# A decoder layer on one core: row maxima of a unit turned by a DMA, and other banks and another order for the background work

## The chip, the cores and the metric

The kernel runs on one core of a Trainium2 chip. The metric is the device time of one execution in microseconds (us), as the median of several executions. Beside it stands one profiled execution, whose trace shows every instruction of the five engines and every DMA. The engines are TensorE (PE in the profile, with its weight loads as PEld), VectorE (DVE), ScalarE (ACT), GpSimd (POOL) and SyncE (SP, which issues the DMAs).

## The reference

One decoder layer in float32 on x of 2 batches x 2048 rows x 512 columns, with 16 heads of width 32. Three sublayers follow each other, each adding to x:

```python
x = x + attn(layernorm(x)) @ W_o.T       # q, k, v by W_q, W_k, W_v; rotary positions on q and k
x = x + gelu(layernorm(x) @ ctx.T) @ ctx # ctx: 77 x 512 for each batch, gelu by tanh
x = x + clip((layernorm(x) @ sign(W).T) * scale + bias, -100, 100)
```

attn is softmax(q k^T / sqrt(32)) v for each head, without a mask, so that every query row meets all 2048 keys of its batch.

## The kernel before, in words

The batches are done one after the other. In each, `project_batch` goes over 16 chunks of 128 rows: layernorm, transpose, the products pk, pq and pv with the three weights (`times`, L179), the rotation (`rotate`), and the transposes of q and k (`transpose_qk`), so that q and k lie with a head's 32 columns on partitions. Then `Attention.run` goes over 32 units. A unit is 256 query rows of four heads, and has 8 steps; a step t takes two chunks of keys, and has two halves, one for heads 0 and 1, one for heads 2 and 3.

The softmax subtracts a row's maximum. These maxima are found ahead, by other matmuls than the ones that are weighed. In each half-step `maxima` (L400) computes two tiles ps of scores with queries on partitions (L412), ten steps ahead (AHEAD), and VectorE reduces them (L424). When a unit's 8 steps of maxima are there, `split_maxima` (L428) takes the negated maximum and splits it into three bf16 parts on GpSimd (casts L433, L435, L437), in a tile mt with queries on partitions. `turn_maxima` (L439) brings them into rows: two TensorE transposes ptm (L443) into a PSUM tile, and a VectorE copy to mrow (L445). The first matmul of a tile of scores, `lower` (L479), multiplies ones by mrow and so puts the negated maxima under the scores (L484; at steps 0 and 4 of each unit). Then come the scores with keys on partitions (L499), which add to what stands there, as the keys of a block are stored as differences to the block before. ScalarE takes the exponent (L625), GpSimd adds pairs for the sums (L627), and TensorE weighs the values (L517) and totals the sums (L531), one and two steps later. `divide` (L541) ends a unit at step 1 of the next: a ScalarE copy, then in each half a VectorE reciprocal (L551) and a GpSimd product.

What follows the attention, `after_attention` (L279), is a generator: output projection and sum with x (po, L293), statistics, the reciprocal root (`rstd_seed`, `rstd_step`), normalization and transpose (pt, L318), the context products (ph, L331; po, L350), the norm again, and the last projection (pf, L358) with scaling, clipping, sum and store. Each yield ends a piece. `background(n)` (L372) takes up to n pieces from the queue. In the attention it is called in the first half of every fourth step and in the second half of each (L635, L644), and in both halves of the last four units; in the projections of the second batch, three pieces at a time. What is left at the very end runs with all generators in turn, and then VectorE does what GpSimd did (`side`).

The order in the attention is the order in the code: a manual schedule covers TensorE, VectorE, ScalarE and GpSimd (L605). It doesn't cover SP, and it doesn't cover the projections and the end, where the planner orders the instructions. Each engine does its instructions in its own order, and so does SP, which holds loads of x, stores of the output and weights in one queue.

[...] ps_t (four, tag t) holds the tiles st of the scores and, in the projections, pt, pk and pq; ps_s (three, tag s) holds the maxima ps, the transposes of q and k, pv, ptm and all tiles of the background; ps_acc has one. A pool hands its banks out in turn, and a tile waits until the one that had its bank before is read.

In the last chunk of a batch (L250 to L270) the products are interleaved with the maxima that are still due (`lead`, L571).

Of the kernel before, what the change touches and what calls it, by code (L numbers as in the profile page):

```python
# [17 lines left out]
P = 128  # L18
B, S, D = 2, 2048, 512
H, DK = 16, 32  # L20
C = 77
# [16 lines left out]
def decoder_layer(  # L38
# [114 lines left out]
    def project_batch(b, ahead, att, wk, wq, wv):  # L153
# [25 lines left out]
        def times(dst, xnt, w, part=range(ND)):  # L179
            for i in part:  # L180
                nc.tensor.matmul(dst, xnt[:, i, :], w[:, i, :], start=(i == 0), stop=(i == ND - 1))  # L181
# [9 lines left out]
            if c == CPB - 1 and 1 in which:  # L191
                att.open_block(blk)

        def values(ch, xnt):
            pv = ps_s.tile([P, D], F32, tag="s", name="pv")
            times(pv, xnt, wv)
            v = kvq.tile([P, D], F32, tag=f"v{ch}", name=f"v_{b}_{ch}")
            nc.scalar.copy(v, pv)
            att.v.append(v)
# [50 lines left out]
        times(pk, xnt, wk)  # L250
        rotate(ch, 1, pk, r)
        transpose_qk(*held)
        values(ch - 1, left)
        transpose_qk(ch, r[:, 0], (1,))
        times(pq, xnt, wq, (0, 1))
        att.lead(1)
        times(pq, xnt, wq, (2, 3))
        rotate(ch, 0, pq, r)
        att.lead(1)
        pv = ps_s.tile([P, D], F32, tag="s", name="pv")  # L260
        times(pv, xnt, wv, (0, 1))
        att.lead(2 * AHEAD)
        times(pv, xnt, wv, (2, 3))
        v = kvq.tile([P, D], F32, tag=f"v{ch}", name=f"v_{b}_{ch}")
        nc.scalar.copy(v, pv)
        att.v.append(v)
        transpose_qk(ch, r[:, 0], (0,))
        att.split_maxima(0)
        att.turn_maxima(0)
# [6 lines left out]
    def side():  # L276
        return nc.vector if alone else nc.gpsimd

    def after_attention(b, blk, ot, first, end):  # L279
        wo, wf, fs, fb = late["wo"], late["wf"], late["fs"], late["fb"]  # L280
        ctxn, ctxt = late["ctx"]
        n = end - first
        chunks = [slice(c * P, (c + 1) * P) for c in range(first, end)]
        whole = slice(first * P, end * P)
        xs = [load_x(b, blk * CPB + c) for c in range(first, end)]
        yield


        def add_to_x(matmuls, mv):
            for c in range(n):  # L290
                ps = ps_s.tile([P, D], F32, tag="s", name="po")
                matmuls(ps, chunks[c])
                nc.vector.tensor_add(xs[c], ps, xs[c])  # L293
                yield
                chunk_stats(xs[c], mv[:, c, :])
                yield


        def norm(mv):
            v, y, t = rstd_seed(mv[:, :, 1], n)  # L300
            yield
            for _ in range(3):
                rstd_step(side(), v, y, t)
                yield
            off = small.tile([P, n], F32, tag=f"off{n}", name="off")
            side().tensor_mul(off, mv[:, :, 0], y)
            side().tensor_scalar(off, off, -1.0, None, ALU.mult)
            yield
            yield
            for c in range(n):  # L310
                xn = work.tile([P, D], F32, tag="w", name="xn2")
                nc.scalar.activation(
                    xn, xs[c], AF.Identity, bias=off[:, c : c + 1], scale=y[:, c : c + 1]
                )
                yield
                pt = ps_s.tile([P, ND, P], F32, tag="s", name="pt2")
                for i in range(ND):
                    nc.tensor.transpose(pt[:, i, :], xn[:, i * P : (i + 1) * P], ident)  # L318
                nc.scalar.copy(ot[:, :, chunks[c]], pt)
                yield  # L320

        def project_out(ps, cols):
            for i in range(ND):
                nc.tensor.matmul(ps, ot[:, i, cols], wo[:, i, :], start=(i == 0), stop=(i == ND - 1))  # L324

        mv = small.tile([P, n, 2], F32, tag=f"mv{n}", name="mv2")
        yield from add_to_x(project_out, mv)
        yield from norm(mv)
        ph = ps_s.tile([C, n * P], F32, tag="s", name="ph")
        for i in range(ND):  # L330
            nc.tensor.matmul(ph, ctxt[:, i, :], ot[:, i, whole], start=(i == 0), stop=(i == ND - 1))  # L331
        h = work.tile([C, n * P], F32, tag="w", name="h")
        nc.scalar.copy(h, ph)
        yield
        u = work.tile([C, n * P], F32, tag="w", name="u")
        side().tensor_mul(u, h, h)
        yield
        side().tensor_scalar(u, u, 0.044715, 1.0, ALU.mult, ALU.add)
        side().tensor_mul(u, u, h)
        yield  # L340
        yield
        nc.scalar.activation(u, u, AF.Tanh, scale=GELU_C)
        yield
        side().tensor_scalar(u, u, 1.0, 0.5, ALU.add, ALU.mult)
        side().tensor_mul(u, u, h)
        yield
        yield

        def attend_ctx(ps, cols):
            nc.tensor.matmul(ps, u[:, cols.start - whole.start : cols.stop - whole.start], ctxn, start=True, stop=True)  # L350

        mv = small.tile([P, n, 2], F32, tag=f"mv{n}", name="mv3")
        yield from add_to_x(attend_ctx, mv)
        yield from norm(mv)
        for c, cols in enumerate(chunks):
            pf = ps_s.tile([P, D], F32, tag="s", name="pf")
            for i in range(ND):
                nc.tensor.matmul(pf, ot[:, i, cols], wf[:, i, :], start=(i == 0), stop=(i == ND - 1))  # L358
            y = work.tile([P, D], F32, tag="w", name="y")
            nc.vector.tensor_mul(y, pf, fs)  # L360
            yield
            side().tensor_add(y, y, fb)
            yield
            side().tensor_scalar(y, y, -MAX_VAL, MAX_VAL, ALU.max, ALU.min)
            side().tensor_add(xs[c], xs[c], y)
            r0 = blk * BLK + (first + c) * P
            nc.sync.dma_start(out[b, r0 : r0 + P, :], xs[c])
            yield

    queue = []  # L370

    def background(n):  # L372
        while queue and n > 0:
            if next(queue[0], queue) is queue:
                queue.pop(0)
            else:
                n -= 1

    def drain():
# [6 lines left out]
    class Attention:  # L386
# [41 lines left out]
        def split_maxima(self, u):  # L428
# [7 lines left out]
            nc.gpsimd.tensor_tensor(neg, neg, mt[:, :, :, 1], ALU.subtract)  # L436
            nc.gpsimd.tensor_copy(mt[:, :, :, 2], neg)  # L437

        def turn_maxima(self, u):  # L439
            mt = mts[u % 2]  # L440
            pt = ps_s.tile([P, 2, P], BF16, tag="s", name="ptm")
            for c in range(2):
                nc.tensor.transpose(pt[:, c, :], mt[:, c].rearrange("p h d -> p (h d)"), ident_b)  # L443
            mrow = small.tile([P, HQ], BF16, tag="mrow", name="mrow")
            nc.vector.tensor_copy(mrow, pt.rearrange("p c q -> p (c q)"))  # L445
            self.mrow[u] = mrow

        def key_steps(self):  # L450
            self.dk = [None] + [
                const.tile([P, ND, BLK], F32, tag=f"w{n}", name=f"dk{n}") for n in "kqv"
            ]

            def differences(g):
                for kb in range(1, NB):
                    nc.gpsimd.tensor_sub(
                        self.dk[kb][:, g, :], self.k[kb][:, g, :], self.k[kb - 1][:, g, :]
                    )
                    yield  # L460

            def others():
                for g in range(1, ND):
                    for _ in differences(g):
                        for _ in range(4):
                            yield

            for _ in differences(0):
                pass
            queue.append(others())  # L470
# [107 lines left out]
        def run(self):  # L578
# [32 lines left out]
                }  # L611
            )
            ordered.__enter__()
            for t in range(NU * STEPS):
                u, i = divmod(t, STEPS)
                pw = big.tile([P, 4, 2, HQ], F32, tag="s", name="pw")
                sm = sums.tile([P, 4, HQ], F32, tag="sm", name="sm")
                for heads, others in (((0, 1), (2, 3)), ((2, 3), (0, 1))):
# [10 lines left out]
                        reduce()  # L629
                    if heads[0] == 0:  # L630
                        first_half()
                        if i == STEPS - 1 and u + 1 < NU:
                            self.turn_maxima(u + 1)
                        finish()
                        if t % 4 == 1 or u >= NU - ND:  # L635
                            background(1)
                    else:
                        finish()
                        second_half()
                        if prev is not None and prev[1] == STEPS - 1:  # L640
                            finish()
                        if (t + AHEAD) % STEPS == STEPS - 1 and u + 1 < NU:
                            self.split_maxima(u + 1)
                        background(1)  # L644
                prev = (u, i, pw, sm)
            first_half()
            second_half()
            while ends:
                finish()
            ordered.__exit__(None, None, None)  # L650

    for b in range(B):
# [60 lines left out]
```

## Time and profile before

| | us |
|---|---|
| median of 3 runs | 2842.28 (2841.74 to 2842.78) |
| profiled execution, its time | 2841.91 |
| profiled execution, its span | 2840.1 |
| TensorE busy in the span | 2800.2 |
| VectorE busy | 1722.5 |
| ScalarE busy | 1321.0 |
| GpSimd busy | 1805.7 |

The span runs from the first to the last instruction. A busy time is the union of an engine's instructions; a matmul's end is modelled, so a matmul that runs slowly and one that is held up can look alike. In the groups, a row names line, engine, operation and tiles, then the count, then busy us and mean ns of one, then the idle time of the engine ahead of it and what ended most of that. In the timeline, a row starts with its start and its duration in us; several like instructions that follow each other are merged, with their count. The granted clock of TensorE was 0.994 in the mean.

From the timeline: the projections of the first batch run to about 229 us, the attention of the first batch to about 1390, the projections of the second to about 1634, its attention to about 2793, and the rest to the end.

### The profile page before, as it was taken

To read this page: it belongs to the slowest core of one execution; us is meant where nothing else is said; L and a number is where in the kernel's file an instruction comes from. 1 tells how busy PE (TensorE), PEld (TensorE's weight loads), DVE (VectorE), ACT (ScalarE), POOL (GpSimd) and SP (SyncE) were. 2 spreads that over 40 slices of the span, in tenths; PEclk is the share of its full clock that TensorE was granted. 3 is DMA by queue.
4 is the path that set the end of the run, shared out by engine and by line. 5 is a ranking of instruction groups with operands and counts; after the bars stand their busy time and mean duration, and the time that the engine had idled before them with its cause. 6 is when DMAs were issued, how large, how long until landed. Compare 5 with 4: busy or idle time off the path is not lost.

```text
span 2840.1 us, 70979 instructions
## 1 busy us (share of the span) xinstructions
PE 2800.2 (99%) x30872; PEld 1494.3 (53%) x30872; DVE 1722.5 (61%) x3065; ACT 1321.0 (47%) x2391; POOL 1805.7 (64%) x2393
## 2 busy tenths in 40 slices
PE   8999999999999999999999999999999999999997
PEld 4445555555555555555444455555555555555554
DVE  4446767666666666665244467766766666666653
ACT  2114555455545544654321155555555455545552
POOL 4326767566856685767654277666677567756772
PEclk9999999999999999999999999999999999999998
DMA  4000000000000010000201000000000000000000
GB/s 135 22 15 1 2 2 2 2 2 9 24 2 2 2 32 1 2 5 28 71 23 34 12 2 2 2 2 2 2 17 17 1 2 9 24 2 2 16 9 15
DMA packets 24007, 39.50 MB, mean 14 GB/s; under 512 B 6902, under 2 KB 6902, under 8 KB 23696
## 3 DMA queue, kind: packets, MB, share of 16 engines
q1 hardware_dynamic: 23696, 34.98, 3.9%
q8 instruction: 241, 3.95, 0.6%
q14 instruction: 70, 0.57, 0.1%
HBM read 26.58 MB, written 8.39 MB: 12 GB/s over the span
## 4 chain that ended last, share of the span: by engine, by line
PE 94%; DVE 2%; POOL 2%; issue 1%; ACT 0%; DMA 0%; ACTq 0%; POOLq 0%; DVEq 0%
PE st L499 20%; PE acc L517 20%; PE ps L412 19%; PE acc L531 8%; PE pf L358 4%; PE po L324 4%; PE pv L181 4%; PE pq L181 4%; PE pk L181 4%; PE st L484 3%; PE pt L318 1%; PE po L350 1%; PE ph L331 1%; PE ptqk L189 1%; DVE mx L424 1%
## 5 line engine op out<-in xcount | busy, mean ns | idle before, releaser
L627 POOL TENSOR_TENSOR sm<-pw 128x512 f32<-128x512 f32 x1024 | 1299.0, 1272 | 665.7 <-ACT pw L625 663.6
L424 DVE TENSOR_REDUCE mx<-ps 128x1 f32<-128x512 f32 x2048 | 1311.6, 682 | 595.1 <-PE ps L412 569.2
L625 ACT ACTIVATE pw<-st 128x512 f32<-128x512 f32 x2048 | 1111.8, 595 | 1038.8 <-PE ps L412 702.5
L412 PE MATMUL ps<-k,q 32*128 32x512 f32 x4096 | 1244.4, 640 | 3.8 <-DVE mx L424 3.5
L517 PE MATMUL acc<-pw,v 128*32 128x256 f32 x8192 | 654.4, 391 | 0.0
L412 PEld LDWEIGHTS ps<-k,q 32*128 32x128 f32 x4096 | 371.7, 183 | 59.3 <-issue 25.8
L531 PE MATMUL acc<-sm,ones 128*32 128x128 f32 x7680 | 388.7, 280 | 1.3 <-POOL sm L627 1.3
L517 PEld LDWEIGHTS acc<-pw,v 128*32 128x32 f32 x8192 | 161.4, 108 | 420.6 <-issue 401.7
L531 PEld LDWEIGHTS acc<-sm,ones 128*32 128x32 f32 x7680 | 247.3, 110 | 156.0 <-POOL sm L627 2.0
L499 PE MATMUL st<-q,dkq 32*128 32x256 f32 x2048 | 294.0, 402 | 0.0
L499 PE MATMUL st<-q,dkk 32*128 32x256 f32 x2048 | 291.3, 400 | 0.0
L499 PE MATMUL st<-q,dkv 32*128 32x256 f32 x2048 | 291.0, 401 | 0.0
L499 PE MATMUL st<-q,k 32*128 32x256 f32 x2048 | 262.8, 374 | 0.0
L499 PEld LDWEIGHTS st<-q,dkk 32*128 32x128 f32 x2048 | 175.2, 184 | 99.5 <-issue 55.5
L499 PEld LDWEIGHTS st<-q,dkq 32*128 32x128 f32 x2048 | 171.3, 184 | 74.1 <-issue 50.9
L499 PEld LDWEIGHTS st<-q,dkv 32*128 32x128 f32 x2048 | 170.4, 184 | 62.6 <-ACT pw L625 26.1
L499 PEld LDWEIGHTS st<-q,k 32*128 32x128 f32 x2048 | 195.2, 187 | 14.2
L214 POOL TENSOR_TENSOR r<-r 128x512 f32<-128x512 f32 x64 | 81.1, 1270 | 184.0 <-DVE r L213 168.4
L293 DVE TENSOR_TENSOR x<-po,x 128x512 f32<-128x512 f32 x64 | 44.2, 691 | 132.4 <-PE po L324 97.7
L190 ACT COPY q<-ptqk 128x512 f32<-128x512 f32 x32 | 18.9, 591 | 221.6 <-PE ptqk L189 221.5
L551 DVE RECIPROCAL num<-num 128x128 f32<-128x128 f32 x128 | 120.5, 942 | 1.8 <-ACT num L545 1.8
L181 PE MATMUL pk<-wk,xnt 128*128 128x512 f32 x256 | 118.6, 606 | 2.0 <-ACT xnt L176 2.0
(100 smaller groups left out, 2085.6 us busy)
## 6 DMA issues: line engine op xcount, KB each, us to landing
x<-in_x_dram SPq DMA_DIRECT2D x64, 256.0 KB, 2.7
out_dram<-x SPq DMA_DIRECT2D x32, 256.0 KB, 2.0
wk<-in_wk_t_dram SPq DMA_DIRECT2D x2, 1024.0 KB, 5.2
wq<-in_wq_t_dram SPq DMA_DIRECT2D x2, 1024.0 KB, 10.1
wv<-in_wv_t_dram SPq DMA_DIRECT2D x2, 1024.0 KB, 9.5
wo<-in_wo_t_dram SPq DMA_DIRECT2D x1, 1024.0 KB, 7.0
wf<-in_wf_t_dram SPq DMA_DIRECT2D x1, 1024.0 KB, 9.0
ctx<-in_ctx_dram SPq DMA_DIRECT2D x2, 154.0 KB
```

The costliest lines, as they stand in the source:

```text
L181: nc.tensor.matmul(dst, xnt[:, i, :], w[:, i, :], start=(i == 0), stop=(i == ND - 1))
L324: nc.tensor.matmul(ps, ot[:, i, cols], wo[:, i, :], start=(i == 0), stop=(i == ND - 1))
L358: nc.tensor.matmul(pf, ot[:, i, cols], wf[:, i, :], start=(i == 0), stop=(i == ND - 1))
L412: nc.tensor.matmul(ps, self.q[qb][self.rows[h], g, q0 : q0 + P], self.k[kb][self.rows[h], g, :], start=True, stop=True,)
L424: nc.vector.tensor_reduce(mx[:, qc, h, kb : kb + 1], ps, AX.X, ALU.max)
L484: nc.tensor.matmul(self.st[h], ones_b[r, :], mrow[r, None, :].to_broadcast([DK, 2, HQ]), start=True, stop=False, skip_group_check=True,)
L499: nc.tensor.matmul(self.st[h][:, c, :], keys[r, g, kc * P : (kc + 1) * P], self.q[qb][r, g, hf * HQ : (hf + 1) * HQ], start=False, stop=Tr ...
L517: nc.tensor.matmul(acc[self.rows[h], 0, :], self.v[self.chunk(i, c)][:, d0 : d0 + DK], pw[:, h, c, :], start=(i == 0 and c == 0), stop=(i ...
L531: nc.tensor.matmul(acc[self.rows[h], 1, part], ones, sm[:, h, part], start=False, stop=(i == STEPS - 1), skip_group_check=True,)
L551: nc.vector.reciprocal(num[:, 1, part], num[:, 1, part])
L625: nc.scalar.activation(pw[:, h], self.st[h], AF.Exp, scale=SCALE)
L627: nc.gpsimd.tensor_add(sm[:, hs, :], pw[:, hs, 0, :], pw[:, hs, 1, :])
```

## The change

Four edits.

1. `turn_maxima` issues one DMA on SP's queue, which transposes both 128x128 bf16 blocks of mt straight to mrow. Only the first unit of each batch keeps the TensorE transposes and the VectorE copy. The call moves from the first half of step 7 to the second half of step 5, right behind `split_maxima`.
2. The tiles of the background come from `bank`: ps_s while the attention runs, ps_t otherwise, and at the very end the two in turn.
3. Each yield of the generator says whether the next piece begins with matmuls of the background. The first half of every odd step takes a piece only if it doesn't (`light`); the second halves and the last four units take any.
4. In the last chunk of a batch, one `lead` follows each of the four matmuls of pq; both pv tiles come from ps_t, and the last is computed in one go after all maxima.

```diff
-        def values(ch, xnt):
-            pv = ps_s.tile([P, D], F32, tag="s", name="pv")
+        def values(ch, xnt, pool=None):
+            pv = (pool or ps_s).tile([P, D], F32, tag="t" if pool else "s", name="pv")
...
-        values(ch - 1, left)
+        values(ch - 1, left, ps_t)
         transpose_qk(ch, r[:, 0], (1,))
-        times(pq, xnt, wq, (0, 1))
-        att.lead(1)
-        times(pq, xnt, wq, (2, 3))
+        for i in range(ND):
+            times(pq, xnt, wq, (i,))
+            att.lead(1)
         rotate(ch, 0, pq, r)
-        att.lead(1)
-        pv = ps_s.tile([P, D], F32, tag="s", name="pv")
-        times(pv, xnt, wv, (0, 1))
         att.lead(2 * AHEAD)
-        times(pv, xnt, wv, (2, 3))
-        v = kvq.tile([P, D], F32, tag=f"v{ch}", name=f"v_{b}_{ch}")
-        nc.scalar.copy(v, pv)
-        att.v.append(v)
+        values(ch, xnt, ps_t)
         transpose_qk(ch, r[:, 0], (0,))
...
+    attending = []
+    banks = [0]
+
+    def bank(shape, name):
+        banks[0] += 1
+        if attending or (alone and banks[0] % 2):
+            return ps_s.tile(shape, F32, tag="s", name=name)
+        return ps_t.tile(shape, F32, tag="t", name=name)
...
             for c in range(n):
-                ps = ps_s.tile([P, D], F32, tag="s", name="po")
+                ps = bank([P, D], "po")
                 matmuls(ps, chunks[c])
                 nc.vector.tensor_add(xs[c], ps, xs[c])
-                yield
+                yield False
                 chunk_stats(xs[c], mv[:, c, :])
-                yield
+                yield c + 1 < n
...
-                yield
-                pt = ps_s.tile([P, ND, P], F32, tag="s", name="pt2")
+                yield True
+                pt = bank([P, ND, P], "pt2")
...
-                yield
+                yield c + 1 == n
...
-    def background(n):
-        while queue and n > 0:
-            if next(queue[0], queue) is queue:
+    heavy = [False]
+
+    def background(n, light=False):
+        while queue and n > 0 and not (light and heavy[0]):
+            more = next(queue[0], queue)
+            if more is queue:
                 queue.pop(0)
+                heavy[0] = False
             else:
+                heavy[0] = more
                 n -= 1
...
         def turn_maxima(self, u):
             mt = mts[u % 2]
-            pt = ps_s.tile([P, 2, P], BF16, tag="s", name="ptm")
-            for c in range(2):
-                nc.tensor.transpose(pt[:, c, :], mt[:, c].rearrange("p h d -> p (h d)"), ident_b)
-            mrow = small.tile([P, HQ], BF16, tag="mrow", name="mrow")
-            nc.vector.tensor_copy(mrow, pt.rearrange("p c q -> p (c q)"))
-            self.mrow[u] = mrow
+            mrow = small.tile([P, 2, P], BF16, tag="mrow", name="mrow")
+            if u > 0:
+                nc.sync.dma_start_transpose(mrow, mt.rearrange("p c h d -> p (c h d)"))
+            else:
+                pt = ps_s.tile([P, 2, P], BF16, tag="s", name="ptm")
+                for c in range(2):
+                    nc.tensor.transpose(
+                        pt[:, c, :], mt[:, c].rearrange("p h d -> p (h d)"), ident_b
+                    )
+                nc.vector.tensor_copy(mrow, pt)
+            self.mrow[u] = mrow.rearrange("p c q -> p (c q)")
...
+            attending.append(True)
             for t in range(NU * STEPS):
...
                         first_half()
-                        if i == STEPS - 1 and u + 1 < NU:
-                            self.turn_maxima(u + 1)
                         finish()
-                        if t % 4 == 1 or u >= NU - ND:
+                        if u >= NU - ND:
                             background(1)
+                        elif t % 2 == 1:
+                            background(1, light=True)
...
                             self.split_maxima(u + 1)
+                            self.turn_maxima(u + 1)
                         background(1)
...
+            attending.clear()
```

More of the change, by code (lines that the diff above doesn't have):

```diff
@@ L285, in after_attention @@
         xs = [load_x(b, blk * CPB + c) for c in range(first, end)]
-        yield
+        yield True
         def add_to_x(matmuls, mv):
             for c in range(n):
-                ps = ps_s.tile([P, D], F32, tag="s", name="po")
+                ps = bank([P, D], "po")
                 matmuls(ps, chunks[c])
                 nc.vector.tensor_add(xs[c], ps, xs[c])
-                yield
+                yield False
                 chunk_stats(xs[c], mv[:, c, :])
-                yield
+                yield c + 1 < n
         def norm(mv):
             v, y, t = rstd_seed(mv[:, :, 1], n)
-            yield
+            yield False
             for _ in range(3):
                 rstd_step(side(), v, y, t)
-                yield
+                yield False
             off = small.tile([P, n], F32, tag=f"off{n}", name="off")
@@ L307, in norm @@
             side().tensor_scalar(off, off, -1.0, None, ALU.mult)
-            yield
-            yield
+            yield False
+            yield False
             for c in range(n):
@@ L314, in norm @@
                 )
-                yield
-                pt = ps_s.tile([P, ND, P], F32, tag="s", name="pt2")
+                yield True
+                pt = bank([P, ND, P], "pt2")
                 for i in range(ND):
@@ L319, in norm @@
                 nc.scalar.copy(ot[:, :, chunks[c]], pt)
-                yield
+                yield c + 1 == n
         def project_out(ps, cols):
@@ L328, in after_attention @@
         yield from norm(mv)
-        ph = ps_s.tile([C, n * P], F32, tag="s", name="ph")
+        ph = bank([C, n * P], "ph")
         for i in range(ND):
@@ L333, in after_attention @@
         nc.scalar.copy(h, ph)
-        yield
+        yield False
         u = work.tile([C, n * P], F32, tag="w", name="u")
         side().tensor_mul(u, h, h)
-        yield
+        yield False
         side().tensor_scalar(u, u, 0.044715, 1.0, ALU.mult, ALU.add)
         side().tensor_mul(u, u, h)
-        yield
-        yield
+        yield False
+        yield False
         nc.scalar.activation(u, u, AF.Tanh, scale=GELU_C)
-        yield
+        yield False
         side().tensor_scalar(u, u, 1.0, 0.5, ALU.add, ALU.mult)
         side().tensor_mul(u, u, h)
-        yield
-        yield
+        yield False
+        yield True
         def attend_ctx(ps, cols):
@@ L355, in after_attention @@
         for c, cols in enumerate(chunks):
-            pf = ps_s.tile([P, D], F32, tag="s", name="pf")
+            pf = bank([P, D], "pf")
             for i in range(ND):
@@ L360, in after_attention @@
             nc.vector.tensor_mul(y, pf, fs)
-            yield
+            yield False
             side().tensor_add(y, y, fb)
-            yield
+            yield False
             side().tensor_scalar(y, y, -MAX_VAL, MAX_VAL, ALU.max, ALU.min)
@@ L367, in after_attention @@
             nc.sync.dma_start(out[b, r0 : r0 + P, :], xs[c])
-            yield
+            yield True
     queue = []
-    def background(n):
-        while queue and n > 0:
-            if next(queue[0], queue) is queue:
+    heavy = [False]
[3 more added lines that the diff above has]
+            if more is queue:
                 queue.pop(0)
+                heavy[0] = False
             else:
+                heavy[0] = more
                 n -= 1
@@ L459, in differences @@
                     )
-                    yield
+                    yield False
             def others():
@@ L465, in others @@
                         for _ in range(4):
-                            yield
+                            yield False
             for _ in differences(0):
```

## The prediction

> **What bounds the kernel now.** I read the page first: the busy times, then the chain that ended last.
>
> ```profile
> PE 2800.2 (99%) x30872; PEld 1494.3 (53%) x30872; DVE 1722.5 (61%) x3065; ACT 1321.0 (47%) x2391; POOL 1805.7 (64%) x2393
> PE 94%; DVE 2%; POOL 2%; issue 1%; ACT 0%; DMA 0%; ACTq 0%; POOLq 0%; DVEq 0%
> ```
>
> The busy row says 99% for TensorE, and the chain agrees. Then the groups by line and shape (count, busy us, mean ns, idle before):
>
> ```profile
> L443 PE MATMUL ptm<-ident_b,mt 128*128 128x128 bf16 x128 | 18.4, 226 | 2.4 <-POOL mt L437 2.4
> L445 DVE COPY mrow<-ptm 128x256 bf16<-128x256 bf16 x64 | 18.0, 282 | 18.8 <-PE ptm L443 18.8
> L551 DVE RECIPROCAL num<-num 128x128 f32<-128x128 f32 x128 | 120.5, 942 | 1.8 <-ACT num L545 1.8
> ```
>
> TensorE sets the end, so only what TensorE does, or waits for, counts. But its busy time hides stalls: an end of a matmul is modelled[...]. So I went on to the timeline and measured from the start of one group of weigh matmuls (L517) to the next: one half-step. First TensorE around a transpose of maxima, then VectorE beside it:
>
> ```profile
> 378.35 0.64 PE L517 MATMUL acc<-pw,v 128*32 128x256 f32 x8
> ...
> 383.96 0.64 PE L517 MATMUL acc<-pw,v 128*32 128x256 f32 x8
> 384.42 0.40 PE L531 MATMUL acc<-sm,ones 128*32 128x128 f32 x8
> 384.75 0.28 PE L443 MATMUL ptm<-ident_b,mt 128*128 128x128 bf16 x2
> 384.97 0.48 PE L499 MATMUL st<-q,dkv 32*128 32x256 f32 x2
> 384.98 0.69 PE L412 MATMUL ps<-k,q 32*128 32x512 f32 x1
> 385.40 0.69 PE L412 MATMUL ps<-k,q 32*128 32x512 f32 x1
> 386.46 0.64 PE L517 MATMUL acc<-pw,v 128*32 128x256 f32 x8
> ```
>
> ```profile
> 384.06 1.29 DVE L424 TENSOR_REDUCE mx<-ps 128x1 f32<-128x512 f32 x2 [0.61 <-PE ps L412]
> 385.27 0.28 DVE L445 COPY mrow<-ptm 128x256 bf16<-128x256 bf16 x1
> ```
>
> This half-step takes 386.46 - 383.96 = 2.50 us; the plain one that starts at 376.45 and ends at 378.35 takes 1.90. Two matmuls of 0.22 us together can't cost 0.60. The rest is a PSUM bank: ps_s has three, the two maxima before hold two until VectorE has reduced them (384.06 to 385.35), ptm takes the third, and the second L412 can't start before 385.40. Where no maxima run any more, ptm costs its own time alone: 2752.54 - 2752.32 = 0.22 us:
>
> ```profile
> 2752.32 0.28 PE L443 MATMUL ptm<-ident_b,mt 128*128 128x128 bf16 x2
> 2752.54 1.13 PE L499 MATMUL st<-q,dkv 32*128 32x256 f32 x8
> ```
>
> [...] The trace of before has no DMA inside SBUF.
>
> **The change, part by part.** Of 64 transposes, 62 leave TensorE (the first of each batch stays). Over all 56 half-steps of the timeline with ptm, four maxima and no other background matmul the mean is 2.52 us, over the 332 plain ones 1.90. So 56 x 0.62 = 34.7 us. The other six: two in the last units at 0.22, two beside a pt at 2.69 - 2.46 = 0.24, two beside a po at 5.64 - 5.49 = 0.15: 1.2 us. **-36 us.** The copy of 282 ns leaves VectorE, which is no bound, and is not counted twice.
>
> What is added: 62 DMA issues on SP, and the wait of the L484 matmuls (the first of a unit) for a landing. Behind that wait all of TensorE stands in order: scores, maxima, weighing; then ScalarE's exponents and GpSimd's sums. What must cover it is the time from GpSimd's last cast to the unit's first L484:
>
> ```profile
> 382.02 0.22 POOL L437 CAST mt<-neg 128x8 bf16<-128x8 f32 x1
> ...
> 387.25 0.39 PE L484 MATMUL st<-mrow,ones_b 32*128 32x512 bf16 x2
> ```
>
> ```profile
> x<-in_x_dram SPq DMA_DIRECT2D x64, 256.0 KB, 2.7
> out_dram<-x SPq DMA_DIRECT2D x32, 256.0 KB, 2.0
> ```
>
> The first fence is the timeline of GpSimd and TensorE, the second the DMA issues with KB and median us to landing. The cover is 387.25 - 382.24 = 5.0 us, less the 0.6 that ptm itself takes: 4.4. I went through the changed order of TensorE and added the background matmuls that lie in between (pt 0.59; po, pf or ph 3.6): of 62 units 20 have 4.4 us, 10 have 5.0, 6 have 5.4, 2 have 5.6, 20 have 8. Four are tight: GpSimd has just written out a chunk (L364 and L365, 1.92 + 1.27 us), the casts come late (last cast ends at 745.67, L484 at 747.80, ptm itself waited 0.59), which leaves about 2.13 - 0.22 - 0.59 = 1.3 us.
>
> The latency L of a transpose is unknown. From below: the store's 2.0 us. From above: [...] the trace's DMA records show the 4,096 64-byte packets of cos and sin in 4.8 us[...]. [...] I take 3.5[...]. Then four units stall 2.2 us: **+9** (2.0: +3; 5: +27, worked as 4 x 3.7 + 20 x 0.6). The DMAs ahead on SP: in the changed order a transpose stands behind a store and a reload of x in six places, where the chunk's last add on GpSimd comes two or more sums (1.27 us each) and the five casts before the transpose is ready, about 3.9 us against some 2.5 for store and reload to issue. So SP blocks nothing, narrowly; were the store late, the six places would cost some 2 us each.
>
> Light pieces move to the first half of odd steps, matmul pieces to second halves. What counts is the half-steps of step 1 of a unit, where VectorE also does a reciprocal (942 ns): with two reduces 1.29 + 0.94 exceeds the half-step (1.64 without L531). Over what the same matmuls take elsewhere, the two half-steps of step 1 and the next one are 0.23, 0.44 and 0.17 us longer in the mean; x 64 this is 53 us. Of it some 9 us come from statistics or a seed beside the reciprocal (6 half-steps at 0.8 over those with a reciprocal alone, 8 after them at 0.48). In the order after, such pairs fall from 18 to 6, and 12 long matmul pieces, which give VectorE time, stand there instead of 8. **-5**, from -9 to +3: ten statistics move to the step right after.
>
> Last projections: L412 waits 0.78 us for a bank in each batch since pv holds one; with pv in ps_t and one lead after every pq matmul that goes, but rotate of q comes later and the casts with it, some 0.3 us back. **-1.** Projections of batch 1: background in ps_t removes waits for banks (1.04 + 0.39 us near 1487), but pk, pq and pt now share four banks with it. **-2**, from -4 to +3. End: one pt (0.6 us) and the first pf move behind the attention, matmul time as before; one ph (1.8 us) now fills part of the 3.98 us wait for xn. **-1**, from -3 to +2.
>
> Sum: -36 + 9 - 5 - 1 - 2 - 1 = -36 us against the profiled execution's 2841.9 (span 2840.1), so 2806; the median of the runs is 2842.3, 0.4 above it. Forecast: **2806 us**.
>
> **Rivals.** (1) The transpose is late everywhere: L over 4.4 us. For: 24 of 62 units have 4.4 us or less[...]. Against: landings of 2.0 to 2.7 with 256 KB, four times this size. The loss is 4(L - 1.3) + 20(L - 4.4) + 10(L - 5) + 6(L - 5.4) + ...; it equals the gains of 45 us at L = 5.5. Between 4.4 and 5.5 it is 2810 to 2842. (2) Slower, by the same term: at L = 7 it is 23 + 52 + 20 + 10 + 3 = 108 us, so 2842 + 63 = 2905 us. It decides from 5.5 on; its place is the idle time before L484. (3) The bank stall stays: after ptm is gone another tile takes its turn in ps_s. Against: plain half-steps with the same two maxima run at 1.86 to 1.90. Then only 62 x 0.22 = 13.6 us go, and with the rest 2828. (4) The reordered background and ps_t collide with VectorE and cost what they should give: +9 instead of -9, 2824.
>
> **How the numbers follow.** 0.62 for the forecast (its own range 2793 to 2816); rival 1 below break-even 0.13; rival 2 0.14; rival 3 0.04; rival 4 0.07. Left out above 2848: nearly all of rival 2 (0.13); below 2790: 0.05, a larger gain from the background. A measurement here tells 0.2% (5.7 us) from no change. Faster: 0.62 + 0.04 + 0.07 + 0.09 of rival 1 = 0.82, less 0.02 for surprises of the order: 0.80. Within 0.2%: 0.05. Slower: 0.15.
>
> **What would show it.** No ptm on TensorE but two; half-steps at step 7 at 1.86 to 1.90 instead of 2.52; L484 preceded by DMA waits in four units of some 2 us, none elsewhere; the transpose listed at about 3.5 us to landing. DMA waits before most L484 mean rival 1 or 2; L412 still held for VectorE at step 7 means rival 3; longer stalls beside L551 mean rival 4. The prediction falls if L is above 5 us, or if SP holds transposes behind loads.

## The result and the profile after

The changed kernel takes **2804.77 us** (median of 4 runs, 2803.13 to 2805.66), against 2842.06 for the kernel before on the same chip (2841.74 to 2842.78). The ratio is 0.9868, with a 95% interval of 0.9851 to 0.9885. The profiled execution took 2803.13 us, with a span of 2801.0. The forecast was 2806 us, with a range of 2790 to 2848.

The page of the kernel after, its busy times and the chain that ended last. TensorE still sets the end:

```profile
PE 2762.5 (99%) x30748; PEld 1490.8 (53%) x30748; DVE 1714.5 (61%) x3003; ACT 1319.9 (47%) x2391; POOL 1804.3 (64%) x2393
PE 96%; DVE 2%; POOL 1%; issue 1%; ACT 0%; DMA 0%; ACTq 0%; DVEq 0%; POOLq 0%
```

The groups by line and shape of the kernel after (count, busy us, mean ns, idle time before). Of the transposes of maxima four matmuls are left, two in each batch, and the first matmul of a unit, L501 (L484 before), waits for no DMA:

```profile
L459 PE MATMUL ptm<-ident_b,mt 128*128 128x128 bf16 x4 | 0.5, 219 | 0.0
L501 PE MATMUL st<-mrow,ones_b 32*128 32x512 bf16 x512 | 99.3, 384 | 0.8 <-DVE mrow L462 0.8
L568 DVE RECIPROCAL num<-num 128x128 f32<-128x128 f32 x128 | 120.5, 943 | 64.2 <-ACT num L562 64.2
```

The timeline of TensorE in the kernel after, at the place where ptm stood (start us, duration us, count at the end). Weighing begins at 376.79 and again at 378.65: the half-step takes 1.86 us, where 2.50 were shown before, and both L423 (L412 before) follow each other without a hole:

```profile
376.79 0.64 PE L534 MATMUL acc<-pw,v 128*32 128x256 f32 x8
...
377.59 0.70 PE L423 MATMUL ps<-k,q 32*128 32x512 f32 x2
...
378.12 0.59 PE L423 MATMUL ps<-k,q 32*128 32x512 f32 x2
...
378.65 0.64 PE L534 MATMUL acc<-pw,v 128*32 128x256 f32 x8
```

The DMA itself: first what the trace answers for the tile mrow (shortest, median and longest, in ns for the issue on SP, in us for the landing), then one of them in the timelines of GpSimd, SP and TensorE:

```profile
L455 SPq DMA_TRANSPOSE mrow<-mt x62: 1168/1169/2458, 252.6 to 2709.6; - x62
DMA to landing us min/median/max: 2.3/2.3/4.0
```

```profile
376.70 0.22 POOL L448 CAST mt<-neg 128x8 bf16<-128x8 f32 x1
...
376.94 1.17 SPq L455 DMA_TRANSPOSE mrow<-mt  x1
...
381.34 0.39 PE L501 MATMUL st<-mrow,ones_b 32*128 32x512 bf16 x2
```

The last cast ends at 376.92, SP issues at 376.94, and TensorE uses mrow at 381.34, 4.42 us after the cast. Over the 62 units this cover is 4.4 us in 30, 3.8 in four, and more in the rest. A landing of 2.3 us fits in everywhere. The trace shows 48 of the 62 landings, the longest of 4.0 us, and none of the 62 made L501 wait.

The spans by stage, from the timeline of TensorE (a stage of attention runs from its first weighing to the end of its last; us):

| | first projections | attention 1 | second projections | attention 2 | end |
|---|---|---|---|---|---|
| before | 234.7 | 1157.3 | 246.8 | 1153.9 | 47.5 |
| after | 231.7 | 1135.7 | 250.8 | 1132.6 | 50.2 |
| transposes alone | 234.9 | 1142.1 | 248.3 | 1138.9 | 45.6 |

In the kernel after, one pt and one pf (0.6 + 3.6 = 4.2 us of matmuls) moved out of each attention into the stage behind it. With this put back, the attentions gained 17.3 and 17.1 us, the first projections 2.9, the second 0.2 and the end 1.5, in all 39.1 (from unrounded times). A gain at the end is no larger than the spread there: the kernel with the transposes alone has the same code at the end as the kernel before, and its end is shorter by almost 2 us.

### The profile page after: what moved, and what is told of

The parts are those of the page before. It is cut to its first block, busy times and chain, and to the rows that moved or that the text cites. A ratio compares the mean times of both kernels' runs of the same rounds, so it can differ in the third digit from the quotient of the medians.

```text
span 2801.0 us, 70846 instructions
## 1 busy us (share of the span) xinstructions
PE 2762.5 (99%) x30748; PEld 1490.8 (53%) x30748; DVE 1714.5 (61%) x3003; ACT 1319.9 (47%) x2391; POOL 1804.3 (64%) x2393
## 2 busy tenths in 40 slices
DMA packets 41864, 43.56 MB, mean 16 GB/s; under 512 B 24759, under 2 KB 24759, under 8 KB 41553
## 4 chain that ended last, share of the span: by engine, by line
PE 96%; DVE 2%; POOL 1%; issue 1%; ACT 0%; DMA 0%; ACTq 0%; DVEq 0%; POOLq 0%
PE st L516 21%; PE acc L534 21%; PE ps L423 18%; PE acc L548 8%; PE pf L363 4%; PE pk L181 4%; PE po L329 4%; PE pv L181 4%; PE pq L181 4%; PE st L501 3%; PE pt L323 1%; PE po L355 1%; PE ph L336 1%; PE ptqk L189 1%; PE pt L174 1%
## 5 line engine op out<-in xcount | busy, mean ns | idle before, releaser
L423 PE MATMUL ps<-k,q 32*128 32x512 f32 x4096 | 1221.6, 639 | 2.2 <-ACT v L198 1.1
L423 PEld LDWEIGHTS ps<-k,q 32*128 32x128 f32 x4096 | 359.4, 183 | 46.7 <-issue 24.3
L516 PEld LDWEIGHTS st<-q,dkv 32*128 32x128 f32 x2048 | 174.7, 184 | 68.8 <-issue 37.3
L568 DVE RECIPROCAL num<-num 128x128 f32<-128x128 f32 x128 | 120.5, 943 | 64.2 <-ACT num L562 64.2
L363 PE MATMUL pf<-wf,q 128*128 128x512 f32 x256 | 119.1, 609 | 0.0
```

Source lines behind the costliest of these rows:

```text
L423: nc.tensor.matmul(ps, self.q[qb][self.rows[h], g, q0 : q0 + P], self.k[kb][self.rows[h], g, :], start=True, stop=True,)
L516: nc.tensor.matmul(self.st[h][:, c, :], keys[r, g, kc * P : (kc + 1) * P], self.q[qb][r, g, hf * HQ : (hf + 1) * HQ], start=False, stop=Tr ...
L568: nc.vector.reciprocal(num[:, 1, part], num[:, 1, part])
```

## The experiments

Two quantities recur. The *cover* of a unit is the time from GpSimd's last cast to the unit's first L501. The *length of a half-step* is the time from one group of weighing matmuls to the next; it is summed over both batches for each place in the unit, some 62 half-steps a place. The runs were made on several chips; the kernel before, run beside each, had medians of 2841.7 to 2842.3 us there. The stages and half-steps come from one profiled execution of each kernel.

**1. The transposes alone.** Edit 1 on the kernel before, nothing else: `turn_maxima` as in the changed kernel, and its call moved:

```diff
-                        if i == STEPS - 1 and u + 1 < NU:
-                            self.turn_maxima(u + 1)
...
                             self.split_maxima(u + 1)
+                            self.turn_maxima(u + 1)
```

> The kernel before, with the transposes of the maxima by DMA alone; background and projections as before. If the transposes cost their bank as well as their own time, this takes nearly all of the gain: the stages of attention have shown 24.9 - 5.3 + 6.3 - 0.3 us of stalls fewer and 13.5 us of own time, 39 in all, so 2803 us. If only their own time counted (62 x 0.22 = 13.6 us) and the other edits brought the rest, it stands at 2828.

Measured: 2810.7 us (2809.3 to 2811.7), 31 of the 37 us, though 8 us above the expected 2803. The half-steps explain the attentions, which took 15.2 and 15.0 us less: the place of ptm (first half of step 7) fell from 166.7 to 131.1 us, the next one rose from 148.2 to 153.5, and all others stayed within 0.1. So taking ptm away gives **-35.6 us**, and something at the start of a unit takes 5.3 back. The groups of this run name it (L489 is that kernel's first matmul of a unit):

```profile
L489 PE MATMUL st<-mrow,ones_b 32*128 32x512 bf16 x512 | 99.5, 385 | 5.9 <-DMA mrow<-mt 5.1 <-DVE mrow L450 0.8
```

**2. A bank taken for nothing.** The changed kernel, with a matmul of 16 columns where ptm stood:

```diff
                         first_half()
+                        if i == STEPS - 1 and u + 1 < NU:
+                            self.hold_bank(u)
                         finish()
...
+        def hold_bank(self, u):
+            r = self.rows[0]
+            pd = ps_s.tile([P, 2, HQ], F32, tag="s", name="pd")
+            nc.tensor.matmul(
+                pd[:, :, 0:8],
+                ones_b[r, :],
+                self.mrow[u][r, None, 0:8].to_broadcast([DK, 2, 8]),
+                start=True,
+                stop=True,
+            )
+            held = small.tile([P, 2, 8], F32, tag="held", name="held")
+            nc.vector.tensor_copy(held, pd[:, :, 0:8])
```

> The changed kernel, and where the transposes of the maxima stood TensorE now does one matmul of 16 columns into a bank of ps_s, and VectorE copies 16 columns of it to a tile that nobody reads: a bank is taken for nothing, with almost no work of TensorE. If the bank was the larger part of a transpose's cost, 0.62 - 0.22 = 0.40 us come back in each of some 58 units: 2805 + 23 = 2828 us. If the cost was TensorE's time, it stays below 2808.

Measured: 2837.05 us (2833.2 to 2837.7), 32 us more. Nearly the whole price of ptm is back without its work: that place in the unit takes 167.4 us, where ptm made it 166.7. The timeline of TensorE in this run:

```profile
380.67 0.64 PE L547 MATMUL acc<-pw,v 128*32 128x256 f32 x8
...
381.46 0.18 PE L470 MATMUL pd<-mrow,ones_b 32*128 32x16 bf16 x1
...
382.65 0.59 PE L423 MATMUL ps<-k,q 32*128 32x512 f32 x1
383.17 0.64 PE L547 MATMUL acc<-pw,v 128*32 128x256 f32 x8
```

The half-step takes 383.17 - 380.67 = 2.50 us, as with ptm. The last L423 starts at 382.65, some 0.6 us later in its half-step than without pd; TensorE counts as busy meanwhile, as the scores (L529) go on at 381.78 and 382.12. VectorE's copy of pd ran from 381.98 to 382.15 and held nothing up: VectorE then idled until its next reduction at 382.68. So the bank was the price, even more than the prediction's split of 0.40 for the bank and 0.22 for the work: with 0.18 us of work that runs beside other matmuls (an L529 starts with pd at 381.46), 31 us in the two attentions over 62 units are 0.5 each.

**3. The order of the pieces undone.** The changed kernel with the calls of before:

```diff
-                        if u >= NU - ND:
-                            background(1)
-                        elif t % 2 == 1:
-                            background(1, light=True)
+                        if t % 4 == 1 or u >= NU - ND:
+                            background(1)
```

> The changed kernel with the order of background pieces in the attention of before (one at every fourth step's first half, heavy or light). By the prediction's term of -5 us for the new order: 2810. By the half-steps of the two traces, where the new order gave 8 us at the reciprocals and took 8 at the seeds of step 3: 2804 to 2805, no change.

Measured: 2807.25 us (2804.36 to 2810.3), by the times between the two theories, and its range overlaps that of the changed kernel. The profiled execution, one of the longer ones, took 2809.15. Its attentions took 1142.3 and 1138.7 us, so that the new order, 4.2 us of moved matmuls put back in each, gives 2.4 and 1.9 there. But it gives them in a way that neither theory had. The group of L501 in this run has 5.1 us of waits for the DMA again, and the timelines of GpSimd and TensorE show one (in brackets the idle time before, and what ended it):

```profile
730.89 1.27 POOL L370 TENSOR_TENSOR x<-x,y 128x512 f32<-128x512 f32 x1
...
734.47 0.22 POOL L448 CAST mt<-neg 128x8 bf16<-128x8 f32 x1
...
737.24 0.39 PE L501 MATMUL st<-mrow,ones_b 32*128 32x512 bf16 x2 [1.20 <-DMA mrow<-mt]
```

GpSimd writes out a chunk (L369, L370) ahead of the casts, these end at 734.69, and the cover without the wait would be 1.35 us. The matmul comes 2.55 us after the cast, so a wait costs 1.2 us. It is the tight unit of the prediction, four times in the program. In the changed order those two instructions come *after* the casts (the last cast ends at 730.74 and L369 starts with its end), and the cover is 3.76 us. So the order of before costs the 5.3 us of experiment 1. Since the new order gives only 4.3 us in the attentions, the rest of it costs about 1; this remainder is a difference of estimates, good to a microsecond or so.

**4 and 5. The transposes issued later.** Split and turn moved from the second half of step 5 to the first half of step 6 (there the same lines stand behind `first_half()`), and to its second half:

```diff
-                        if (t + AHEAD) % STEPS == STEPS - 1 and u + 1 < NU:
+                        if i == STEPS - 2 and u + 1 < NU:
                             self.split_maxima(u + 1)
                             self.turn_maxima(u + 1)
```

> The changed kernel with the split of the maxima and their transpose called one half-step later (first half of step 6 instead of second half of step 5), so that the time from GpSimd's last cast to the unit's first lowering matmul is shorter by 1.86 us: some 2.5 us in 30 units, 1.9 in 4, more in the rest. Where TensorE had to wait in the run with the transposes alone, a cast was followed by its matmul after 2.5 to 2.7 us. So by that measure 0 to 0.1 us in 30 units and 0.7 in 4: 2805 to 2811 us. If a transpose took the 3.5 us of the prediction: 30 x 1.0 + 4 x 1.6 = +36, 2841.

> The same two half-steps later (second half of step 6): cover of about 0.65 us in 30 units, 0.05 in 4, 1.9 in 2, 2.9 to 4.9 in the rest. If all of TensorE stands behind the wait, 30 x 1.9 + 4 x 2.5 + 2 x 0.7 = 68 us come on top: 2873. If other matmuls fill the wait, or VectorE and GpSimd catch up in it what they are behind: a half of that or less, below 2840.

Measured: 2838.78 us (2835.3 to 2842.0) and 2925.01 (2891.8 to 2942.1; its profiled execution 2891.82). So all of TensorE does stand behind the wait, as the rivals had it, but my two expectations were low for two reasons.

The first is that 2.4 us of cover aren't safe. In the run a half-step later, TensorE sat idle before L501 in 18 units, where the changed kernel has no such gap. Four of these had the writing of a chunk ahead of the casts again, with 13.2 us in all. The other 14 waited 13.5 us together, 0.3 to 1.9 each; the longest belong, as far as the trace shows it, to landings of 3.6 to 4.3 us instead of 2.3. The second is the clock. TensorE's timeline at one of the four, and then windows of the same run (from and to, length, busy us of each engine with counts, then the granted clock of TensorE as a share of full speed, and two columns on DMA):

```profile
2444.87 0.61 PE L501 MATMUL st<-mrow,ones_b 32*128 32x512 bf16 x2 [3.38 <-DMA mrow<-mt]
```

```profile
2445.00:2450.00 5.00, 5.00 (x42) 3.15 (x42) 1.29 (x2) 1.08 (x2) 2.02 (x2) 0.50 0.01 3
2450.00:2455.00 5.00, 5.00 (x68) 2.48 (x66) 3.20 (x5) 2.76 (x5) 1.80 (x2) 0.94 0.00 0
```

TensorE idles for 3.38 us, and for the next 5 us the granted clock is 0.50, then 0.94, as it is full again from 2450.6 on. So this gap cost about 3.4 + 0.50 x 5 + 0.06 x 5 = 6.2 us, an estimate. The slow clock lasted some 6 us beyond the gap in three of the four and 3.3 in the first. The four (13.2 us idle, some 11 of slow clock) and the 13.5 us of other waits make 38; the span grew by 36. The four gaps are of 3.2 to 3.4 us. In the run a step later the clock was 0.50 for 3.4 us at two of the five gaps of 2.0 to 2.3 us (2.18 and 2.22), and experiment 12 shows such a stretch beside an idle time of 0.8; how long TensorE must idle for it, these runs do not show. With the later call the profiled execution waited in 46 units, 75 us in all, and its clock was 0.50 for 27 us of the attentions, which by the same estimate costs up to 14 more; its span grew by 88.7. The other executions of that kernel took 31 to 50 us more, at a mean granted clock of 0.971 to 0.979 instead of 0.992; why it differs from one to the next is open.

**6. Seeds in another shape.** In the changed order the seed of the reciprocal root falls to step 3, and the half-steps there grew. The timelines of VectorE and GpSimd in the kernel after:

```profile
534.49 0.16 DVE L135 TENSOR_SCALAR v<-mv 128x4 f32<-128x4 f32 x1
534.68 1.18 DVE L138 TENSOR_SCALAR t<-v 128x4 int32<-128x4 int32 x1
...
534.56 1.27 POOL L645 TENSOR_TENSOR sm<-pw 128x512 f32<-128x512 f32 x1 [0.74 <-ACT pw L643]
```

A VectorE instruction on four columns takes 1.18 us and ends at 535.86 beside a sum of GpSimd that ends at 535.83; of the 54 seed instructions on two or four columns, all 13 that started during a sum took 0.60 to 1.28 us, and the 41 that started with GpSimd idle at most 0.17. The next reductions start only at 535.98, and TensorE's weight load for an L423 at 536.71 has 0.42 us of idle time ahead of it that one of them ended. That the layout of source and destination decides was a guess, which no trace had shown. To test it, the same three instructions were laid out as 3 by 2 columns with a gap on one side, against 6 in a row on the other:

```diff
+        v = small.tile([P, 3, 4], F32, tag="v3", name="v")[:, :, :2]
+        y = small.tile([P, 3, 4], F32, tag="rstd3", name="rstd")[:, :, :2]
+        t = small.tile([P, 3, 2], F32, tag="t3", name="t")
         nc.vector.tensor_scalar(v, var, 1.0, EPS, ALU.mult, ALU.add)
...
-            v, y, t = rstd_seed(mv[:, :, 1], n)
+            v, y, t = seed_apart(mv[:, :, :, 1], n)
...
```

> The changed kernel with the seed of the reciprocal root in the background laid out so that source and destination of each of its three VectorE instructions have different outer sizes (3 by 2 columns with a gap on one side, 6 in a row on the other)[...]; two spare columns ride along, and one memset a chunk group is added. [...] none is longer than 0.3 us and the 8 us at step 3 go: 2797 to 2799. If they are slow for another reason[...], the long ones stay: 2805 to 2807.

Measured: 2798.7 us (2795.2 to 2800.8), 6 us less, and the second half of step 3 fell from 174.7 to 167.4 us. All 66 seed instructions take 161 ns or less, also the 26 that started during a sum of GpSimd. The timelines of VectorE and GpSimd, the same chunk as above:

```profile
534.00 0.16 DVE L155 TENSOR_SCALAR t<-v 128x6 int32<-128x6 int32 x1
...
533.89 1.27 POOL L662 TENSOR_TENSOR sm<-pw 128x512 f32<-128x512 f32 x1 [0.74 <-ACT pw L660]
```

VectorE's instruction starts 0.11 us into the sum and isn't held. Engine, operations, place and neighbour are the same, so the shape decides. By what mechanism it does, no trace shows.

**7. Reciprocals in quarters.**

```diff
-            for c in range(2):
-                part = slice(c * P, (c + 1) * P)
+            w = P if last else P // 2
+            for c in range(HQ // w):
+                part = slice(c * w, (c + 1) * w)
                 nc.vector.reciprocal(num[:, 1, part], num[:, 1, part])
...
```

> The changed kernel with the reciprocals of a unit in four pieces of 64 columns over four half-steps, instead of two of 128 over two. If the 45 us of stalls at steps 1 and 2 come from one reciprocal of 0.94 us and two reductions of 1.29 us not fitting a half-step, a piece of about 0.5 us leaves 0.15 us over in the two half-steps without totals and nothing after: 26 to 35 us go, 2770 to 2779. If only VectorE's total time mattered: no change or a little slower, 2805 to 2808.

Measured: 2789.71 us (2789.0 to 2790.7), 15 less where 26 to 35 were expected: the stall was from the reciprocals, but only in part. Its group row has the piece:

```profile
L569 DVE RECIPROCAL num<-num 128x64 f32<-128x64 f32 x252 | 136.2, 542 | 45.1 <-ACT num L562 45.1
```

The second half of step 1 fell from 161.1 to 143.8 us and the next from 132.8 to 129.2, but the first half of step 1 stayed at 120.5. There no reciprocal is in the way: a half-step without totals takes 1.64 us elsewhere (386.48 to 388.12 in this run's timeline) and 1.90 there (384.58 to 386.48), and its last L423 starts at 385.96, as VectorE ends the reductions of the pair before (384.68 to 385.97). Step 3 lost 3 us: its first half rose from 121.7 to 126.0. It did so too in experiment 8, where no seed is held, so the seeds aren't the reason; which wait it is stays open.

**8 to 10. Both, and the banks undone.** Seeds in the other shape and quarters together; the same with ps_s for the background at all times; and that last edit alone on the changed kernel:

```diff
-        if attending or (alone and banks[0] % 2):
+        if True:
             return ps_s.tile(shape, F32, tag="s", name=name)
```

> The changed kernel with both edits: the seeds in the other shape, and the reciprocals in four pieces. If each takes away its own stalls (the seeds in step 3, where the run with quarters spent 10 us more than the run with the other shape; the reciprocals 15 us in steps 1 and 2), it stands at 2790 - 10 = 2780 us. If both drew on the same slack of VectorE, the second gives little: 2785 to 2789.

> The same with all tiles of the background in the banks of the scores, at all times. If the 2 us by which that was ahead of the changed kernel belong to it: 2 us below the other run of this call. If it was the spread between runs: within 1 us of it.

> The changed kernel with all tiles of the background in the three banks of the scores, at all times. By the prediction (-2 us in the second projections and part of -1 at the end): 2807 to 2808. By the stages of the two traces (0.5 us in the second projections and 1.7 at the end, both with a matmul's work moved there taken off): 2807. If banks outside the attention do nothing: 2805.

Measured: 2779.44 us (2778.5 to 2780.6) with both edits, and **2776.74** (2776.0 to 2777.8) with the banks of the scores as well, 0.9771 of the kernel before (0.9758 to 0.9784). On the changed kernel alone the banks of the scores gave 2802.57 (2801.1 to 2803.95), 2.2 less. So the edits to seeds and reciprocals add up: in the attentions of the profiled executions both took 27 us off, and alone 9 and 17. By the medians it is 25 against 6 and 15; the rest lies outside the attention and is not explained. The edit to the banks costs 2 to 3 us: the two ranges with both edits don't overlap, those on the changed kernel just do.

**11 and 12. Where the banks cost, and the last projections.** On the kernel with both edits: the banks undone at the end only, and, in another kernel, the last projections of a batch as before, the banks of pv among them.

```diff
-        if attending or (alone and banks[0] % 2):
+        if attending or alone:
```

```diff
-        values(ch - 1, left, ps_t)
+        values(ch - 1, left)
...
-        for i in range(ND):
-            times(pq, xnt, wq, (i,))
-            att.lead(1)
-        rotate(ch, 0, pq, r)
-        att.lead(2 * AHEAD)
-        values(ch, xnt, ps_t)
+        times(pq, xnt, wq, (0, 1))
+        att.lead(1)
+        times(pq, xnt, wq, (2, 3))
+        rotate(ch, 0, pq, r)
+        att.lead(1)
+        pv = ps_s.tile([P, D], F32, tag="s", name="pv")
+        times(pv, xnt, wv, (0, 1))
+        att.lead(2 * AHEAD)
+        times(pv, xnt, wv, (2, 3))
...
```

> The kernel with the other shape and the quarters (2779.4 us), and at the end of the program, after all attention, only the banks of the scores for the background; the second projections keep the other banks. All banks undone gave 2.7 us. If these lie at the end: 2777. If they lie in the second projections: 2779 to 2780.

> The same kernel (2779.4 us) with the last projections of each batch in the order and the banks of before. The stage of the first projections was 234.7 and 234.9 us in the two runs with that order and 231.0 to 231.7 in all others, so 3.3 us there and as much or less in the second batch: 2782.5 to 2786. By the prediction's term of 1 us: 2780.4.

Measured: 2778.61 us (2777.9 to 2779.1), so of the 2.7 us some 0.8, no more than the spread of the runs, lie at the end and the rest in the second projections, whose stage is 2.5 us shorter in the profiled execution of experiment 9 than in that of experiment 8 (250.0 against 252.5); which wait there I have not isolated. And 2784.99 (2783.0 to 2786.6), so the order and the banks of the last projections are worth **5.5 us** by the medians, not 1; the profiled executions differ by 3.4, with 2.2 in the first projections and 1.6 in the second. The groups in the stretch of 200 to 236 us, in the run with the old order and in the one with the new:

```profile
L198 PE MATMUL pv<-wv,xnt 128*128 128x512 f32 x16 | 9.2, 718 | 0.0
```

```profile
L198 PE MATMUL pv<-wv,xnt 128*128 128x512 f32 x16 | 7.3, 599 | 0.0
```

Sixteen matmuls at 718 ns in place of 599 are 1.9 us that the profile counts as busy. They are not waits: in the run with the old order four of the sixteen took 0.93 to 1.22 us each and the others 0.59 to 0.70, and the four lie where the granted clock was 0.50 (from 225.1 to 228.5). The windows of both runs, as in experiments 4 and 5, first the old order, then the new (the clock is the third number from the end):

```profile
220.00:230.00 10.00, 8.84 (x28) 3.61 (x30) 4.27 (x9) 1.07 (x2) 3.52 (x7) 0.83 0.00 0
```

```profile
220.00:230.00 10.00, 9.62 (x55) 4.58 (x52) 5.59 (x12) 2.16 (x4) 4.87 (x9) 1.00 0.00 0
```

All three profiled executions with the old order (before, experiment 1 and this one) have such a stretch of 3.4 or 6.8 us here, behind an idle time of TensorE of 0.78 us, and none of the eleven with the new order has one. In the second projections of this run the same idle time stands, the clock is full and pv takes 603 ns in the mean, so the idle time alone doesn't bring the slow clock; what does is open.

## Why the prediction was right, step by step

- **-36 for ptm: right.** -35.6 by experiment 1. The bank's share was nearly all (experiment 2), and the rival that it stays (2828) fell.
- **+9 for four late transposes: the mechanism was right, the place was gone.** Two terms failed. The latency taken, 3.5 us, was an estimate, as the trace of before has no such DMA; measured are 2.3 to the landing in most, 2.55 from cast to use. By the packet counts of the two profile pages (24,007 before, 41,864 after) each of the 62 transposes makes 288. And the cover of 1.3 us was read from the trace of before, whose order put the writing of a chunk ahead of the casts. I went through TensorE's changed order for the other units, but not GpSimd's for these four. The count of the others was off as well: 30 units have a cover of 4.4 us, not 20. With the old order the term is +5.3 (1.35 us of cover, as predicted); in the changed kernel it is 0. The +9 came from a wrong latency and an outdated order, and that the sum was right in spite of it is luck.
- **-5 for the new order of the pieces: wrong sign, about +1.** Beside reciprocals it did give 8 us: those three places together fell from 53.3 to 45.2 us over what their matmuls take elsewhere. But I did not price a seed at step 3, where its long instructions cost 7 us (experiment 6, 174.7 against 167.4). What made the new order worth having was the late transposes that it avoids, 5.3 us, which I had not connected with it.
- **-1 for the last projections: mis-sized, -5.5.** I priced the 0.78 us of idle time that a row showed. Beside it the durations of pv were longer, as the granted clock was 0.50 there for 6.8 us in the kernel before (from 223.9) and for 3.4 in the second projections (from 1630.2); in the kernel after it is full at both places. I had not looked at the clock of that stretch. Part of the 5.5 us is not explained.
- **-2 and part of -1 for other banks outside the attention: wrong sign, +2 to +3.** The prediction itself named what may stand behind it, "pk, pq and pt now share four banks"; which of these tiles waits is not shown.
- **The end:** about -1.5 in the stage of the profiled execution, as large as the runs' spread.
- **SP blocks nothing: right.** Each transpose was issued 0.03 us after its cast.
- **Rivals 1 and 2, a late transpose:** they needed more than 4.4 us, and the longest landing in the trace was 4.0. Experiments 4 and 5 show that the mechanism is real where the cover is shorter, and dearer than priced.
- **Rival 4, background and banks that collide:** half of it came true. Those two terms are +3.5 instead of -7, beside a larger gain elsewhere.

With the measured terms, -35.6 + 0 + 1 - 5.5 + 2.5 is -37.6, and the median fell by 37.3. The small terms are good to a microsecond or two each, and -5.5 was measured on a kernel with two more edits, so that a closer agreement than that is chance. The forecast of 2806 came out close because errors cancelled: 9 us of late transposes that didn't come and 4.5 us missed at the last projections stood against 6 us too hopeful for the order and some 4.5 for the banks.

## What to carry to other kernels

Price a tile in PSUM by the bank that it takes from a rotation, not by the instruction that writes it: a matmul of 16 columns cost as much as two full transposes (167.4 us at that place in the unit, against 166.7; 131.1 with neither). A DMA that must land before the bottleneck engine goes on needs its cover worked out in the *changed* order of every engine ahead of it, and cover beyond the median landing: with 2.4 us of cover and a median landing of 2.3, 14 units still waited 13.5 us. Where a row shows an idle time, as the 0.8 us in the last projections, look also at whether the durations beside it are longer than elsewhere (718 ns for pv against 599), and then at the granted clock of that stretch (0.50 there) before you call them waits.

## What the runs showed of the hardware

- VectorE's tensor_scalars of the seed on two or four columns took 0.60 to 1.28 us where they started during a GpSimd sum (13 of 13, kernel after), and at most 0.17 with GpSimd idle (41 of 41). With outer sizes of 3 on one side and 6 on the other they took at most 0.16, also during a sum (26 of 26, experiment 6).
- At four idle gaps of TensorE of 3.2 to 3.4 us (experiment 4) the granted clock was 0.50 for 6.8 us, or 3.4 at one of the four. It was 0.50 for 3.4 us also at two of five gaps of 2.0 to 2.3 us (experiment 5), and for 3.4 in the last projections of experiment 12 beside an idle time of 0.8.
- A transpose of 128 x 256 bf16 inside SBUF by DMA took 1.17 us to issue on SP in the median and landed after 2.3 us in the median. In the kernel after, eight of the 48 landings in the trace took 2.5 to 4.0 us; SP had issued no other DMA within 12 us of these. In experiment 4 the longest was 4.3.
